# Attention times a gated FFN on one core: the place where softmax rows are divided by their sums, the engine that makes p's low part, and two narrow matmuls

## The chip, the cores and the metric

The kernel runs on one core of one Trainium2 chip. The metric is the device time of one launch in microseconds; the kernel before took 1223.08 us, the median of three runs (1222.31 to 1223.10). One more execution was taken with the hardware profiler. Engines are named as in the profile: PE is TensorE's matmul, PEld its weight load, DVE is VectorE, ACT is ScalarE, POOL is GpSimd, SP is SyncE, which here only issues transfers.

## The reference

x has 4 batches of 512 rows with 512 columns; there are 16 heads of 128 columns, and an FFN with 1408 inner columns whose weights are small integers (-1, 0, 1).

```python
xn = layernorm(x)                                  # no scale, no shift
q, k, v = (xn @ W + b for each of 16 heads)
scores = q @ k.T / sqrt(128), causal mask
attn = softmax(scores)                             # rows sum to 1
z = attn @ v
s = sum over heads of z @ W_O + b_O
g = silu(down(silu(xn @ gate * gate_s) * (xn @ up * up_s)) * down_s)
out = x + s * g
```

## The kernel before

Nearly every matrix is held as a high and a low part in a rounded 32-bit format (`Split`), and a product of two such matrices is three matmuls: high by low, high by high and low by high (`mm3`, lines 91 to 93). The high part is a cast, mostly on ACT, and the low part is the difference between the source and the high part, mostly on DVE; the low parts of the attention weights are made on POOL (`split_w`, line 135).

First the 512 rows of batch 0 are normalised and transposed. The later batches go the same way inside the first heads (`ln_stats`, `ln_normalize`, `ln_transpose`, `ln_low`).

Then the loop `heads` runs over 64 pairs of head and batch, n = 0 to 63: groups of two heads outermost (8 groups), the 4 batches next, the two heads of the group innermost (i = 0 and 1). The order of instructions is written out by hand. In one iteration TensorE does, in this order: the scores of this head (`softmax`, three packs of row tiles: the fourth, the third, the second with the first), two fillers (`fill`: for i = 0 the value projections psv of this batch and group, for i = 1 the output products pso of the previous one), the projections psq and psk for the next head, the value product of the previous head (`attend`, lines 376 to 393), and the other two fillers. So the probabilities of a head are used one iteration after they are made.

Between the scores and the value product, p goes this way. DVE masks, scales and takes the row maximum (L298); ACT exponentiates and sums the row (L312); DVE takes the reciprocal of the sum (L315) and POOL multiplies the row by it (L316). The row tiles are kept packed without the masked upper triangle: 10 tiles of 128x128. p has to be transposed: DVE transposes 32x32 blocks (L330, `turn_p`), one store writes them to device memory ("turn", L335) and four loads bring them back in the transposed order ("ptr", L341), all issued by SP. In the next iteration `split_p` makes the high part on ACT (L357) and the low part on DVE (L358), in two halves of 128x640 each. In the first heads (n < 4) and in the last iteration `split_p` stands right behind `softmax`, in the others behind the first fillers and the turn. For the very last head, TensorE transposes p instead (`transpose_p`, L370 and L372), as no iteration is left to hide the way through memory.

The value product has, for each of the four key tiles j, the rows from tile j on: widths 512, 384, 256 and 128. Each of the three parts (high by high, low by high, high by low) takes the four tiles, in the order 0, 3, 1, 2, into one PSUM tile z: 12 matmuls. ACT then adds the bias and rounds (L391, high part of z) and DVE makes the low part (L392).

The weights of the next group arrive through a pool of four raw buffers (`rawp`), by loads that ACT issues (L130), and are split when due (`split_pending`); q's and k's weights are split in the iterations n = 6, 14, ... (and 7, 15, ...). From group 1 on an output product adds to what is already in memory: ACT issues the load of it (L401), DVE adds (L413), SP issues the store (L414). ACT also issues loads of the FFN weights that are only examined (`load_look`, `look`).

PSUM has a ring of 3 buffers for scores and transposes (`ps_st`) and one of 5 for everything else (`ps_mm`): psq, psk, psv, pso, z, and half of the transposes of LN. A head takes seven buffers of the second ring.

After the last head come its value product, the four last output products, and the FFN: its weights are loaded by transfers that POOL issues (L651), gate and up products and then the down product for each batch.

Of the kernel before, what the change touches and what calls it, by code (L numbers as in the profile page):

```python
# [18 lines left out]
P = 128  # L19
HG = 2  # L20
# [22 lines left out]
def kernel(  # L43
# [21 lines left out]
    nc = tc.nc  # L65
    B, S, D = x.shape
# [29 lines left out]
    with ExitStack() as at:  # L96
# [111 lines left out]
        def ln_normalize(b, t):  # L208
            xt = x_in.pop((b, t))
            mv, sd = ln_of.pop((b, t))  # L210
            rstd = small.tile([P, 1], F32, name="rstd")
            nc.vector.reciprocal(rstd, sd)
            xn = lnp.tile([P, D], F32, name="xn")
            nc.vector.tensor_scalar(xn, xt, mv[:, 0:1], rstd, ALU.subtract, ALU.mult)
            xn_of[b, t] = xn

        def ln_transpose(b, t):
            xn = xn_of.pop((b, t))
# [53 lines left out]
        def softmax(qT, kT):  # L272
            p = pp.tile([P, NS * P], F32, name="p", tag="p")
            of = [p[:, row[t] : row[t] + (t + 1) * P] for t in range(NT)]
            nmax = {}
            for pack in PACK:
                sc = ps_st.tile([P, S], F32, name="sc", tag="st")
                at_ = 0
                where = {}
                for t in pack:  # L280
                    n = (t + 1) * P
                    where[t] = sc[:, at_ : at_ + n]
                    if t > 0:
                        mm3(where[t], qT[:, ts(t, P)], kT[:, :n], True, True)
                    at_ += n
                if 0 in pack:

                    two = sc[:, at_ - P : at_ + P]
                    nc.tensor.matmul(two, qT.hi[:, :P], kT.both[:, :, :P], start=True, stop=False)
                    nc.tensor.matmul(where[0], qT.lo[:, :P], kT.hi[:, :P], start=False, stop=True)  # L290
                for t in pack:
                    n = (t + 1) * P
                    add = mask[:, S - n :]
                    if t == 0:
                        add = small.tile([P, P], F32, name="add", bufs=1)
                        nc.vector.tensor_tensor(add, two[:, P:], mask[:, S - P :], ALU.add)
                    nmax[t] = small.tile([P, 1], F32, name="nmax", bufs=8)
                    nc.vector.tensor_tensor_reduce(  # L298
                        out=of[t],
                        in0=where[t],  # L300
                        in1=add,
                        scale=-SCALE,
                        scalar=BIG,
                        op0=ALU.add,
                        op1=ALU.min,
                        accum_out=nmax[t],
                    )
            for pack in PACK:
                for t in pack:
                    tot = small.tile([P, 1], F32, name="tot", bufs=8)  # L310
                    rtot = small.tile([P, 1], F32, name="rtot", bufs=8)
                    nc.scalar.activation(  # L312
                        of[t], of[t], AF.Exp, bias=nmax[t], scale=-1.0, accum_out=tot
                    )
                    nc.vector.reciprocal(rtot, tot)  # L315
                    nc.gpsimd.tensor_scalar(of[t], of[t], rtot, 1.0, ALU.mult, ALU.mult)  # L316
            return of

        def turn_p(of):

# [22 lines left out]
                )  # L343
            return raw

        def split_p(raw):
            pt = weight(pp, [P, NS, P], "pt", "pt")
            half = NQ // 2
            for k in range(0, NQ, half):
                src = raw[:, k : k + half].rearrange("p b (s i) -> p b s i", i=Q)  # L350

                def dst(part):
                    return part[:, :, k * Q : (k + half) * Q].rearrange(
                        "p s (b i) -> p b s i", i=Q
                    )

                nc.scalar.copy(dst(pt.hi), src)  # L357
                nc.vector.tensor_tensor(dst(pt.lo), src, dst(pt.hi32), ALU.subtract)  # L358
            return pt

        def transpose_p(of):

            pt = weight(pp, [P, NS, P], "pt", "pt")
# [12 lines left out]
        def attend(h, pt, vs):  # L376
            z = ps_mm.tile([P, NT, P], F32, name="z", tag="mm")


            todo = []  # L380
            for part, other in (("hi", "hi"), ("lo", "hi"), ("hi", "lo")):
                for j in (0, NT - 1, 1, 2):
                    v = getattr(vs[j], part)[:, ts(h % HG, E)]
                    p_ = getattr(pt, other)[:, slot[j] : slot[j] + NT - j, :]
                    todo.append((z[:, j:, :], v, p_))
            for k, (o, v, p_) in enumerate(todo):
                nc.tensor.matmul(o, v, p_, start=k == 0, stop=k == len(todo) - 1)  # L387
            zT = weight(zp, [P, NT, P], f"z{h}", "z")

            bias = bv_sb[:, h : h + 1]  # L390
            nc.scalar.activation(zT.hi, z, AF.Identity, bias=bias)  # L391
# [69 lines left out]
        with tc.manual_schedule():  # L461
# [56 lines left out]
            zs = {}  # L518
            inexact, before, raw = None, None, None

            def attend_last(before, pt):
                g, b, i = before
                zs.setdefault((g, b), []).append(attend(g * HG + i, pt, v_of[g, b]))

            for n, (g, b, i) in enumerate(heads):
                h = g * HG + i
# [22 lines left out]
                of = softmax(qT, kT)  # L549
                if n > 1 and early:  # L550
                    pt = split_p(raw)
                look()
# [1 line left out]
                fill(range(0, half))  # L554
                if nxt is not None:
                    raw_next = turn_p(of)
                if not early:
                    pt = split_p(raw)
                split_pending(n)
# [36 lines left out]
                    *_, kT = project(nxt[1], nh, wk[nh], bk_sb, "k")  # L596
                    raw = raw_next
                if before is not None:
                    attend_last(before, pt)
# [17 lines left out]
                before = g, b, i  # L617
# [6 lines left out]
            zs[last].append(attend(H - 1, pt, v_of[last]))  # L624
            for t in range(NT):
                project_out(*last, t, zs[last])

# [176 lines left out]
```

## Time and profile before

| what | value |
| --- | --- |
| median of three runs | 1223.08 us |
| the profiled execution | 1222.41 us |
| its span, from the first to the last instruction | 1220.6 us |
| scaling of p on POOL (L316) | 256 instructions, 598 ns mean |
| reciprocals on DVE (L315) | 256 instructions, 162 ns mean |
| low part of p on DVE (L358) | 126 instructions, 1099 ns mean |
| high part of p on ACT (L357) | 126 instructions, 724 ns mean |
| transposes of p on DVE (L330) | 378 instructions, 361 ns mean |
| packets below 512 bytes | 13232 of 117912 |
| mean transfer rate | 177 GB/s |

The span is the part of the execution between the first and the last instruction that the profile shows, and some 1.8 us lie around it. Busy time is the sum over an engine's instructions; matmuls overlap one another, so what a matmul costs is the distance between two starts and not its duration. A line of the timeline gives the start, the duration, the engine, the source line, the operation, what it writes and reads, and, in square brackets, the idle time of the engine just before it and what ended that.

### The profile page before, as it was taken

What the parts mean: (1) busy time and instruction counts of PE and PEld (TensorE: products, weight loads), DVE (VectorE), ACT (ScalarE), POOL (GpSimd) and SP (SyncE); (2) the same over time, 40 slices, a digit from 0 to 9 for tenths busy, and PEclk for the clock granted to TensorE, in tenths of its full rate; (3) what the DMA queues carried; (4) which work ended last, traced back from release to release, by engine and by line L of the source; (5) the groups of instructions that cost most, each with busy time, mean ns of one, the idle gap of its engine ahead of it and who ended that gap; (6) DMA issues with size and microseconds to landing.
All of it is one profiled execution on the core that took longest, in us unless ns stands there. A gap on an engine that the chain in (4) does not pass through costs nothing.

```text
span 1220.6 us, 18887 instructions
## 1 busy us (share of the span) xinstructions
PE 1206.5 (99%) x6514; PEld 1052.7 (86%) x6514; DVE 827.1 (68%) x2044; ACT 525.3 (43%) x1169; POOL 301.7 (25%) x433
## 2 busy tenths in 40 slices
PE   8999999999999999999999999999999999999997
PEld 8888888888888888888888888888888888888886
DVE  6897777777777777777877676767677533434343
ACT  5654444444445445444544454445444342323231
POOL 4212321232123213321412141214121341212010
PEclk9999999999999999999999999999999999999999
DMA  4454456656665667566655565555544893627241
GB/s 161 138 175 147 145 165 206 206 179 190 190 207 174 203 198 218 181 208 192 211 182 173 178 189 175 177 185 173 173 156 156 272 317 93 207 87 213 80 147 38
DMA packets 117912, 215.55 MB, mean 177 GB/s; under 512 B 13232, under 2 KB 45744, under 8 KB 117808
## 3 DMA queue, kind: packets, MB, share of 16 engines
q1 hardware_dynamic: 74016, 134.51, 34.4%
q10 hardware_dynamic: 29376, 53.26, 14.2%
q0 software_dynamic: 14416, 26.48, 7.9%
q8 instruction: 53, 0.87, 0.3%
q14 instruction: 51, 0.42, 0.1%
HBM read 135.17 MB, written 79.04 MB: 175 GB/s over the span
## 4 chain that ended last, share of the span: by engine, by line
PE 95%; DVE 3%; ACT 1%; DMA 0%; issue 0%; SPq 0%; DVEq 0%; ACTq 0%
PE z L387 10%; PE pd L667 7%; PE pg L667 7%; PE pu L667 7%; PE pso L91 5%; PE psv L91 5%; PE pso L92 5%; PE pso L93 5%; PE psv L93 5%; PE psv L92 5%; PE psq L91 5%; PE psq L92 5%; PE psq L93 5%; PE psk L91 5%; PE psk L92 5%; PE psk L93 5%
## 5 line engine op out<-in xcount | busy, mean ns | idle before, releaser
L316 POOL TENSOR_SCALAR p<-p,rtot 128x512 f32<-128x512 f32 (+3 forms) x256 | 148.2, 598 | 675.1 <-DVE rtot L315 675.1
L312 ACT ACTIVATE p<-p,nmax 128x512 f32<-128x512 f32 (+3 forms) x256 | 140.9, 552 | 147.3 <-DVE nmax L298 147.3
L358 DVE TENSOR_TENSOR ptl<-ptr,pth 128x640 fp32r<-128x640 f32 x126 | 133.7, 1099 | 1.4 <-ACT pth L357 1.4
L330 DVE STREAM_TRANSPOSE sq<-p 128x256 f32<-128x256 f32 x378 | 113.3, 361 | 0.0
L298 DVE CUSTOM_DVE_ANT_0 p<-sc,mask 128x512 f32<-128x512 f32 (+2 forms) x192 | 96.5, 552 | 0.3 <-PE sc L93 0.3
L252 ACT ACTIVATE k<-psk,consts 128x512 fp32r<-128x512 f32 (+1 forms) x65 | 44.2, 681 | 108.7 <-PE psk L93 108.6
L252 ACT ACTIVATE q<-psq,consts 128x512 fp32r<-128x512 f32 (+1 forms) x65 | 44.3, 682 | 97.2 <-PE psq L93 72.6
L357 ACT CAST pth<-ptr 128x640 fp32r<-128x640 f32 x126 | 84.9, 724 | 0.1
L413 DVE TENSOR_TENSOR a<-pso,a 128x512 f32<-128x512 f32 x108 | 72.1, 686 | 17.7 <-PE pso L93 16.4
L255 DVE SCALAR_TENSOR_TENSOR k<-psk,consts,k 128x512 fp32r<-128x512 f32 (+1 forms) x65 | 48.0, 739 | 52.8 <-ACT k L252 52.7
L693 DVE SCALAR_TENSOR_TENSOR hd<-pu,consts,sg 128x512 f32<-128x512 f32 x44 | 33.0, 751 | 66.8 <-PE pu L667 62.2
L315 DVE RECIPROCAL rtot<-tot 128x1 f32<-128x1 f32 x256 | 41.6, 162 | 42.7 <-ACT p L312 36.3
L91 PE MATMUL sc<-k,q 128*128 128x512 f32 (+2 forms) x192 | 65.7, 342 | 1.7 <-DVE xl L225 1.7
L93 PE MATMUL sc<-k,q 128*128 128x512 f32 (+2 forms) x192 | 64.7, 337 | 0.0
L92 PE MATMUL sc<-k,q 128*128 128x512 f32 (+2 forms) x192 | 64.7, 337 | 0.0
L255 DVE SCALAR_TENSOR_TENSOR q<-psq,consts,q 128x512 fp32r<-128x512 f32 (+1 forms) x65 | 47.6, 732 | 7.6 <-ACT q L252 7.6
L312 ACT ACTIVATION_READ_ACCUMULATOR p<-p,nmax 128x1 f32 x256 | 47.8, 187 | 0.0
L91 PEld LDWEIGHTS sc<-k,q 128*128 128x128 f32 x192 | 36.2, 188 | 7.9 <-DVE xl L225 3.5
L723 ACT ACTIVATE o<-o 128x512 f32<-128x512 f32 (+1 forms) x17 | 10.3, 607 | 68.8 <-DVE o L722 68.8
L92 PEld LDWEIGHTS sc<-k,q 128*128 128x128 f32 x192 | 36.2, 189 | 3.6
L93 PEld LDWEIGHTS sc<-k,q 128*128 128x128 f32 x192 | 36.1, 188 | 2.6
L691 ACT ACTIVATE sg<-pg,consts 128x512 f32<-128x512 f32 x44 | 30.3, 688 | 17.0 <-PE pg L667 17.0
(734 smaller groups left out, 3811.6 us busy)
## 6 DMA issues: line engine op xcount, KB each, us to landing
turn<-sq SPq DMA_DIRECT2D x63, 640.0 KB, 3.8
ptr<-turn SPq DMA_DIRECT2D x252, 160.0 KB, 3.4
acc<-a SPq DMA_DIRECT2D x124, 256.0 KB, 3.7
a<-acc ACTq DMA_DIRECT2D x108, 256.0 KB, 2.8
xt<-in_x SPq DMA_DIRECT2D x16, 256.0 KB, 4.1
wor<-in_w_o ACTq DMA_DIRECT2D x16, 256.0 KB, 4.5
fa<-acc SPq DMA_DIRECT2D x16, 256.0 KB, 5.9
fx<-in_x SPq DMA_DIRECT2D x16, 256.0 KB, 6.9
```

Of the source, the lines that this page charges most:

```text
L91: nc.tensor.matmul(ps, a.hi, b.lo, start=first, stop=False)
L92: nc.tensor.matmul(ps, a.hi, b.hi, start=False, stop=False)
L93: nc.tensor.matmul(ps, a.lo, b.hi, start=False, stop=last)
L252: nc.scalar.activation(q.hi[:, at_], ps[:, at_], AF.Identity, bias=bias[:, h : h + 1])
L255: nc.vector.scalar_tensor_tensor(q.lo[:, at_], ps[:, at_], bias[:, h : h + 1], q.hi32[:, at_], ALU.add, ALU.subtract,)
L298: nc.vector.tensor_tensor_reduce(out=of[t], in0=where[t], in1=add, scale=-SCALE, scalar=BIG, op0=ALU.add, op1=ALU.min, accum_out=nmax[t],)
L312: nc.scalar.activation(of[t], of[t], AF.Exp, bias=nmax[t], scale=-1.0, accum_out=tot)
L316: nc.gpsimd.tensor_scalar(of[t], of[t], rtot, 1.0, ALU.mult, ALU.mult)
L330: nc.vector.transpose(dst.rearrange("p a s i -> p s a i"), src.rearrange("p (s a i) -> p s a i", s=n, i=Q),)
L358: nc.vector.tensor_tensor(dst(pt.lo), src, dst(pt.hi32), ALU.subtract)
L387: nc.tensor.matmul(o, v, p_, start=k == 0, stop=k == len(todo) - 1)
L667: nc.tensor.matmul(ps, l, r, start=first and k == 0, stop=last and k == len(pairs) - 1)
```

## The change

Four things change.

p is no longer divided by its row sums. The four sums of a head are collected in one tile `tot`, one reciprocal is taken of all four, and the result is stored to a small memory tile in the order of the rows and loaded back as a row of 512 values that is repeated on all 128 partitions (`load_rtot`). The value product, whose columns are the query rows, is multiplied by it (`zn`), before bias and rounding.

p's low part is made on POOL instead of DVE. The high and low part now lie side by side in one tile (`p_split`).

The last key tile's matmuls leave the PSUM tile z. v's high part by both parts of p is one matmul of 256 columns, and v's low part by p's high part one of 128, into a tile z2 of its own; ACT copies z2 to the SBUF and DVE adds its two halves and then z. The other nine matmuls go in the order of the tiles.

The normalised rows of LN are written over x's tile instead of into one of their own.

```diff
-            xn = lnp.tile([P, D], F32, name="xn")
-            nc.vector.tensor_scalar(xn, xt, mv[:, 0:1], rstd, ALU.subtract, ALU.mult)
-            xn_of[b, t] = xn
+            nc.vector.tensor_scalar(xt, xt, mv[:, 0:1], rstd, ALU.subtract, ALU.mult)
+            xn_of[b, t] = xt
...
+            tot = small.tile([P, NT], F32, name="tot", bufs=2)
             for pack in PACK:
                 for t in pack:
-                    tot = small.tile([P, 1], F32, name="tot", bufs=8)
-                    rtot = small.tile([P, 1], F32, name="rtot", bufs=8)
                     nc.scalar.activation(
-                        of[t], of[t], AF.Exp, bias=nmax[t], scale=-1.0, accum_out=tot
+                        of[t], of[t], AF.Exp, bias=nmax[t], scale=-1.0,
+                        accum_out=tot[:, t : t + 1],
                     )
-                    nc.vector.reciprocal(rtot, tot)
-                    nc.gpsimd.tensor_scalar(of[t], of[t], rtot, 1.0, ALU.mult, ALU.mult)
-            return of
+            rtot = small.tile([P, NT], F32, name="rtot", bufs=2)
+            nc.vector.reciprocal(rtot, tot)
+            by_tile = dram.tile([NT, P], F32, name="rtot_d", tag="rtot_d", bufs=2)
+            nc.sync.dma_start(out=by_tile.rearrange("t p -> p t"), in_=rtot)
+            return of, by_tile
+
+        def load_rtot(by_tile):
+
+            r = small.tile([P, NT, P], F32, name="rb", bufs=2)
+            row_ = by_tile.rearrange("t p -> (t p)").rearrange("(o n) -> o n", o=1)
+            nc.sync.dma_start(
+                out=r.rearrange("p t q -> p (t q)"), in_=row_.broadcast_to([P, NT * P])
+            )
+            return r
...
+        def p_split():
+            both = pp.tile([P, 2, NS, P], F32R, name="pt", tag="pt")
+            pt = Split(both[:, 0], both[:, 1])
+            pt.both = both
+            return pt
...
                 nc.scalar.copy(dst(pt.hi), src)
-                nc.vector.tensor_tensor(dst(pt.lo), src, dst(pt.hi32), ALU.subtract)
+                nc.gpsimd.tensor_tensor(dst(pt.lo), src, dst(pt.hi32), ALU.subtract)
...
-        def attend(h, pt, vs):
+        def attend(h, pt, vs, rb):
             z = ps_mm.tile([P, NT, P], F32, name="z", tag="mm")
+            z2 = ps_mm.tile([P, 2, P], F32, name="z2", tag="mm")
+            last = NT - 1
+            e = ts(h % HG, E)
...
             for part, other in (("hi", "hi"), ("lo", "hi"), ("hi", "lo")):
-                for j in (0, NT - 1, 1, 2):
-                    v = getattr(vs[j], part)[:, ts(h % HG, E)]
+                for j in range(last):
+                    v = getattr(vs[j], part)[:, e]
...
+            s_ = slot[last]
+            nc.tensor.matmul(z2, vs[last].hi[:, e], pt.both[:, :, s_, :], start=True, stop=False)
+            nc.tensor.matmul(z2[:, 0], vs[last].lo[:, e], pt.hi[:, s_, :], start=False, stop=True)
+            zn = zp.tile([P, NT, P], F32, name="zn", bufs=1)
+            rest = small.tile([P, 2, P], F32, name="rest", bufs=1)
+            nc.scalar.copy(rest, z2)
+            nc.vector.tensor_tensor(rest[:, 0], rest[:, 0], rest[:, 1], ALU.add)
+            nc.vector.tensor_tensor(zn[:, last], z[:, last], rest[:, 0], ALU.add)
+            nc.vector.tensor_tensor(zn[:, :last], z[:, :last], rb[:, :last], ALU.mult)
+            nc.vector.tensor_tensor(zn[:, last], zn[:, last], rb[:, last], ALU.mult)
             zT = weight(zp, [P, NT, P], f"z{h}", "z")
...
-            nc.scalar.activation(zT.hi, z, AF.Identity, bias=bias)
-            nc.vector.scalar_tensor_tensor(zT.lo, z, bias, zT.hi32, ALU.add, ALU.subtract)
+            nc.scalar.activation(zT.hi, zn, AF.Identity, bias=bias)
+            nc.vector.scalar_tensor_tensor(zT.lo, zn, bias, zT.hi32, ALU.add, ALU.subtract)
...
                 if nxt is not None:
                     raw_next = turn_p(of)
+                rb_next = load_rtot(sums)
                 if not early:
                     pt = split_p(raw)
```

The sums' store is issued by SP behind the exponentials and ahead of the turn store of the same head; the repeated load behind the four ptr loads.

More of the change, by code (lines that the diff above doesn't have):

```diff
@@ L344, in turn_p @@
             return raw
+        def p_split():
[3 more added lines that the diff above has]
+            return pt
         def split_p(raw):
-            pt = weight(pp, [P, NS, P], "pt", "pt")
+            pt = p_split()
             half = NQ // 2
@@ L357, in split_p @@
                 nc.scalar.copy(dst(pt.hi), src)
[L358 removed]
+                nc.gpsimd.tensor_tensor(dst(pt.lo), src, dst(pt.hi32), ALU.subtract)
             return pt
         def transpose_p(of):
[L363 removed]
+            pt = p_split()
             pairs = [(j, t) for j in range(NT) for t in range(j, NT)]
@@ L519, with attend_last @@
             inexact, before, raw = None, None, None
-            def attend_last(before, pt):
+            def attend_last(before, pt, rb):
                 g, b, i = before
-                zs.setdefault((g, b), []).append(attend(g * HG + i, pt, v_of[g, b]))
+                zs.setdefault((g, b), []).append(attend(g * HG + i, pt, v_of[g, b], rb))
             for n, (g, b, i) in enumerate(heads):
@@ L548 @@
                     pt = split_p(raw)
-                of = softmax(qT, kT)
+                of, sums = softmax(qT, kT)
                 if n > 1 and early:
@@ L598 @@
                 if before is not None:
-                    attend_last(before, pt)
+                    attend_last(before, pt, rb)
                 if n == 1:
@@ L616 @@
                     fill(range(half, NT))
-                before = g, b, i
+                before, rb = (g, b, i), rb_next
                 if n == len(heads) - 4:
@@ L623 @@
             last = (NG - 1, B - 1)
-            zs[last].append(attend(H - 1, pt, v_of[last]))
+            zs[last].append(attend(H - 1, pt, v_of[last], rb))
             for t in range(NT):
```

## The prediction

> **What bounds the kernel now.** First the page's busy shares, then the chain of waits by engine:
>
> ```profile
> PE 1206.5 (99%) x6514; PEld 1052.7 (86%) x6514; DVE 827.1 (68%) x2044; ACT 525.3 (43%) x1169; POOL 301.7 (25%) x433
> ...
> PE 95%; DVE 3%; ACT 1%; DMA 0%; issue 0%; SPq 0%; DVEq 0%; ACTq 0%
> ```
>
> then the stage windows; this row covers some 16 of the 64 heads (n = 0 to 63; value products start 14.8 us apart); after the window stand its length and PE's busy time:
>
> ```profile
> 400.00:640.00 240.00, 240.00 (x1346) 212.17 (x1346) 183.66 (x468) 109.40 (x258) 64.72 (x80) 1.00 0.64 199
> ```
>
> TensorE is busy 240 of 240 us at full granted clock. So only two things count: TensorE work added or removed, and new TensorE stalls. DVE, ACT and POOL have room on average; I ask where a result of theirs now comes later than TensorE has work to bridge.
>
> **TensorE work.** One value product in the timeline (start, duration):
>
> ```profile
> 505.45 0.39 PE L387 MATMUL z<-pth,v_0h 128*128 128x512 f32 x1
> 505.68 0.22 PE L387 MATMUL z<-pth,v_3h 128*128 128x128 f32 x1
> 505.73 0.39 PE L387 MATMUL z<-pth,v_1h 128*128 128x384 f32 x1
> ...
> 507.36 0.28 PE L91 MATMUL psv<-wv4l,xh 128*128 128x256 f32 x1
> ```
>
> Durations overlap; the price is the pitch from start to start. The block takes 507.36 − 505.45 = 1.91. Pitches: 512 wide 0.23, 384 0.17, 256 0.12. A 128-wide matmul gives 0.055 here and makes the next one 0.055–0.06 later (its weight load isn't covered), together 0.115. The change turns three 128-wide ones into one 256-wide and one 128-wide: 3 × 0.115 − 0.118 − 0.115 = 0.11 a head. Four of 64 lie inside the stalls below: 60 × 0.112 = **−6.7 us**.
>
> **Other engines, per head.** POOL loses four scalings of p (598 ns mean, 2.1–2.5 us together) and gets two low parts of 128x640. The trace has no such POOL op; the nearest row is its 128x512 subtraction (second line: beside a DVE subtraction):
>
> ```profile
> 472.81 1.29 POOL L135 TENSOR_TENSOR wq8l<-wqr,wq8h 128x512 fp32r<-128x512 f32 x1 [1.49 <-ACT wq8h L134]
> 474.06 1.88 POOL L135 TENSOR_TENSOR wk8l<-wkr,wk8h 128x512 fp32r<-128x512 f32 x1
> ```
>
> By elements, 640/512 × 1.25 (pitch) = 1.57, the pair 3.15. Lower end: 2 × 1.25 = 2.5, if the instruction counts more than its elements; upper end: 640/512 × 1.88 = 2.35, the pair 4.7, if something beside it stretches it as the second line was. DVE loses 1.52 (the subtraction) and three of four reciprocals (3 × 0.16), and gets four operations after z: by its 128x128 add (0.29) and 128x384 and 512 rows (0.55, 0.69), 1.4. ACT gets one 128x256 copy (0.37). The copy, the four operations and their handovers put z's high part 2.4 us after the last matmul instead of 0.7, its low part 3.1 instead of 1.5, and each engine works in order: casts of v and additions of the output queued behind z come up to 1.7 later. The prediction rests on POOL's price, and here a rule speaks against the change. The Trainium skill, "GPSIMD Engine Reference", § 3.1 Elementwise, puts a two-input operation at about 2.6 cycles an element on GpSimd against one on DVE, and keeps elementwise work on DVE. By the row, 1.29 against DVE's 0.69 for 512, POOL takes 3.15; by the rule's 2.6 × 1.52, 4.0, an estimate. With 4.0 every stall below that waits for POOL grows by 0.85: 9 × 0.85 = 7.6 us more, an end of about 1234. I take the row.
>
> In most heads I expect no wait from either: in head 16 POOL's pair starts when ACT's first cast of p ends, 501.2, and ends at 504.4, and the z matmul that reads it, the seventh, comes at 506.6; z is read by the output product a head later; z's own PSUM buffer, the first of them to be used again, is due some 6 us on. Without that cover each us late is one us a head. Three places differ.
>
> **1. Heads 6, 14, ... 54 (seven).** Here POOL also makes wq's and wk's low parts (the two lines above), and ACT's queue holds loads that wait for their raw buffers:
>
> ```profile
> 471.49 0.73 ACT L357 CAST pth<-ptr 128x640 fp32r<-128x640 f32 x1
> ...
> 474.14 0.34 ACTq L130 DMA_DIRECT2D wqr<-in_w_q  x1
> 475.97 0.34 ACTq L130 DMA_DIRECT2D wkr<-in_w_k  x1
> 476.35 0.44 ACTq L438 DMA_DIRECT2D look<-in_up_w  x1
> 476.85 0.69 ACT L252 ACTIVATE q<-psq,consts 128x512 fp32r<-128x512 f32 x1 [3.59 <-PE psk L93]
> ```
>
> The load of wkr goes at 475.97, when POOL ends wk's low part (475.94); the cast of q stands behind it, so the releaser named, psk, is not what ended the wait. Now POOL does p's pair first: 471.73 to 474.87, then wq 1.25 to 476.12, wk 1.25 to 477.37 (nothing on DVE is beside it any more); q's high part 478.28, its low part until about 479.74. Before, that was hidden: no buffer was due. Now z2 takes an eighth PSUM buffer per head from a ring of five, so the second matmul group after z (due at 479.24) gets psq's buffer, released by q's low part: stall about 0.5. 7 × 0.5 = **+3.4 us**. With POOL's lower end nothing; with its upper end 0.5 + 1.55 = 2.05 a head.
>
> **2. The early heads (n = 1 to 3).** DVE runs from z0 without a gap into the next LN statistics and softmax:
>
> ```profile
> 46.32 0.69 DVE L187 BATCH_NORM_STATS2 st<-xt 128x6 f32<-128x512 f32 x1
> ...
> 49.52 0.66 DVE L298 CUSTOM_DVE_ANT_0 p<-sc,mask 128x512 f32<-128x512 f32 x1
> ```
>
> z0's longer chain moves all by 1.5. The exponentials and the cast of p follow, so z1 starts 1.5 later; POOL's pair then ends at 58.9, and the seventh matmul waits 1.3 more. q, LN, k, z1 and xl on DVE follow, and the third score product, which waits for xl already,
>
> ```profile
> 65.36 0.39 PE L91 MATMUL sc<-k,q 128*128 128x256 f32 x1 [0.41 <-DVE xl L225]
> ```
>
> comes at 68.15: **+2.8 us**; head 3 on has room.
>
> **3. The tail.** POOL's last pair ends at 962.3, where the seventh matmul was due at 961.66 (the new, shorter block wants it at 961.42); the casts for the last head's transposed p stand behind z14's longer chain on ACT, and the last value product ends at 968.45 instead of 966.70. Then nothing but one z14 group is left to cover z15's chain:
>
> ```profile
> 966.89 0.69 ACT L391 ACTIVATE z15h<-z,consts 128x512 fp32r<-128x512 f32 x1 [2.48 <-PE z L387]
> ```
>
> The first product with z15 went at 967.64, 0.94 after the block; now 2.45 after it: 970.9, **+3.25 us**.
>
> **Hidden.** The sums' 512-element store and 256 KB broadcast load go on SP: the store ahead of the turn store, the load behind the four ptr loads. Turn and ptr:
>
> ```profile
> turn<-sq SPq DMA_DIRECT2D x63, 640.0 KB, 3.8
> ptr<-turn SPq DMA_DIRECT2D x252, 160.0 KB, 3.4
> ```
>
> In head 16 ptr is issued until 508.36, lands about 511.8, and is needed at 514.17: 2.4 us of slack cover a delay. No row shows a store of single 4-byte elements; nearest by its kind is the 256 KB acc store, 3.7 to landing. The Trainium skill, "DMA: Bandwidth & Descriptors", § Rules for kernel authors, speaks against it: a last dimension that isn't contiguous goes as one descriptor an element, 512 here, and should be rearranged. By the row it lands 3.7 after its issue, which stands some 3 us ahead of the turn store, and turn loses under 1 us; by the rule it is dearer, without a price. Between nothing and 5 us I take the row: hidden. Beyond the slack every head pays (rival D). LN in place makes the next x load wait for the transposes instead of the normalising, far ahead of its use. The first FFN weight loads, behind POOL's last p work at 961.20, move past z15's chain too; the first lands some 2.6 us before its use: 0, at worst 1.
>
> **Sum.** −6.7 + 2.8 + 3.4 + 3.25 = +2.75 us on the profiled 1222.41: 1225.2; on the median of the three runs, 0.7 above that execution, 1225.8; I say **1226**. No change is within 0.2%, 2.45 us.
>
> **Rivals.**
> A, as summed, with its own range 1222 to 1231: 0.50.
> B, the other side: the stalls are covered. POOL's pair takes 2.6 or less, so that psq's buffer is free in time, and the early DVE queue catches up. Left are −6.7 + 2.5 of tail: 1219. It decides when POOL's chain in head 14 is 0.5 us shorter. For it: averages with much room. Against: POOL's row, and nothing shorter on it. 0.27.
> C, POOL's 32-element runs cost more than its contiguous row, 1.5 × 1.57 (the upper end): 7 × 2.05 + 4.35 + 4.8 − 6.7 = +16.8, 1240. DVE's pair shows no such penalty (0.76 each against 0.69 for 512). 0.13.
> D, the small store delays turn by over 2.4 us beyond its slack: each us is 60 us, 1280. 0.06.
> E, the joined matmul saves nothing, because its weight load stays exposed: +9.5, 1233. The 256-wide pitch 0.12 beside a 384 one speaks against. 0.04.
>
> The range 1220 to 1235 leaves out C, D and the lower part of B. Faster by over 0.2% (below 1220.6): 0.17 of B. Slower (above 1225.5): C, D, E and 0.32 of A, 0.55 in all. The rest, 0.18 of A and 0.10 of B, is 0.28.
>
> **What would show it.** Right: a z block of 1.80; waits of psv for q's low part in heads 6, 14, ...; a wait on POOL in the z block near 57 and 961; the third score product at 68. Wrong: POOL's op far from 1.57; a wait of pth for ptr; no stall in head 14.

## The result and the profile after

The changed kernel takes 1510.61 us (median of six runs, 1499.24 to 1521.22), the kernel before 1222.97 beside it: ratio 1.2355, 95% interval 1.2288 to 1.2422. The profiled execution has a span of 1518.1 us. The page of the changed kernel, busy shares, packets and the chain of waits by engine:

```profile
PE 1308.4 (86%) x6450; PEld 1103.4 (73%) x6450; DVE 746.8 (49%) x1982; ACT 541.5 (36%) x1233; POOL 330.0 (22%) x303
...
DMA packets 160921, 232.47 MB, mean 153 GB/s; under 512 B 48048, under 2 KB 80560, under 8 KB 160816
...
DMA 45%; PE 28%; DVE 11%; ACT 6%; SPq 3%; POOL 3%; issue 2%; ACTq 1%; DVEq 0%; POOLq 0%
```

TensorE, 95% of the chain before, is 28% of it now; transfers are 45%. The stage windows show TensorE idle for 54 of 300 us in the middle heads, at a granted clock of 0.91:

```profile
500.00:800.00 300.00, 246.15 (x1224) 207.64 (x1223) 148.87 (x422) 106.48 (x256) 65.15 (x46) 0.91 0.82 156
```

The transfers by kind (count, KB each, median us to landing) say which:

```profile
turn<-sq SPq DMA_DIRECT2D x63, 640.0 KB, 13.0
ptr<-turn SPq DMA_DIRECT2D x252, 160.0 KB, 3.4
acc<-a SPq DMA_DIRECT2D x124, 256.0 KB, 10.9
a<-acc ACTq DMA_DIRECT2D x108, 256.0 KB, 12.4
rb<-rtot_d SPq DMA_DIRECT2D x64, 256.0 KB, 4.6
...
rtot_d<-rtot SPq DMA_DIRECT2D x64, 2.0 KB, 12.7
```

The smallest store of the program, 2 KB, takes 12.7 us, and what starts beside it is late as well: turn lands in 13.0 us instead of 3.8, the loads of the output sums, which ACT issues, in 12.4. ptr and rb are issued when it is over, and ptr lands as before. The loads of the output sums in the kernel before:

```profile
a<-acc ACTq DMA_DIRECT2D x108, 256.0 KB, 2.8
```

One head in SP's timeline of the changed kernel:

```profile
587.50 0.38 SPq L318 DMA_DIRECT2D rtot_d<-rtot  x1
587.93 0.98 SPq L444 DMA_DIRECT2D acc<-a  x2
589.01 0.44 SPq L346 DMA_DIRECT2D turn<-sq  x1
603.29 1.91 SPq L352 DMA_DIRECT2D ptr<-turn  x4
```

turn goes out 1.5 us behind the store and ptr 14.3 us behind turn, because it reads what turn wrote. From there two ways lead to TensorE. The waits of the engines (total in us, times, longest):

```profile
ACT pt L374 <- DMA ptr<-turn: 189.4, 47, 11.8
...
ACT q L251 <- DMA rtot_d<-rtot: 105.2, 11, 10.4
...
PE z L407 <- ACT pt L374: 65.9, 34, 7.2
PE pso L91 <- DVE q L254: 62.5, 12, 6.4
...
PE z L407 <- POOL pt L375: 41.5, 43, 1.3
```

The first way is the long one, by turn and ptr: the casts of p wait for ptr, and the value product z waits for p's two parts. The second goes through ACT's own order. In the head shown ACT has cast p by 591.58 and issued four loads by 592.85, and then it stands until a load of FFN weights goes out at 601.21; q's cast comes behind that load:

```profile
601.64 0.69 ACT L251 ACTIVATE q<-psq,consts 128x512 fp32r<-128x512 f32 x1 [10.06 <-DMA rtot_d<-rtot]
```

The trace puts this wait down to the 2 KB store itself, which lands at 601.19. The load doesn't touch what the store writes; in the trace both report their landing on one semaphore (the counter that tells that a transfer is done), and the load's issue waits for it. TensorE waits for q's low part, and after the wait goes on slowly:

```profile
596.64 0.39 PE L93 MATMUL pso<-wo3h,z7l 128*128 128x512 f32 x1
603.17 0.80 PE L91 MATMUL pso<-wo3l,z6h 128*128 128x512 f32 x1 [6.14 <-DVE q L254]
603.76 0.63 PE L92 MATMUL pso<-wo3h,z6h 128*128 128x512 f32 x1
604.19 0.63 PE L93 MATMUL pso<-wo3h,z6l 128*128 128x512 f32 x1
```

Matmuls of 512 columns are 0.43 us apart there instead of 0.23, and TensorE stays slow for some 6 us: from 603.10 to 609.10 its granted clock is 0.52.

### The profile page after: what moved, and what is told of

It reads as the page before. It is cut to its first block, busy times and chain, and to the rows that moved or that the text cites. A ratio compares the mean times of both kernels' runs of the same rounds, so it can differ in the third digit from the quotient of the medians.

```text
span 1518.1 us, 18901 instructions
## 1 busy us (share of the span) xinstructions
PE 1308.4 (86%) x6450; PEld 1103.4 (73%) x6450; DVE 746.8 (49%) x1982; ACT 541.5 (36%) x1233; POOL 330.0 (22%) x303
## 4 chain that ended last, share of the span: by engine, by line
DMA 45%; PE 28%; DVE 11%; ACT 6%; SPq 3%; POOL 3%; issue 2%; ACTq 1%; DVEq 0%; POOLq 0%
DMA turn<-sq 23%; DMA rtot_d<-rtot 10%; PE pd L698 5%; PE pg L698 5%; PE pu L698 5%; DMA ptr<-turn 5%; DMA a<-acc 5%; DVE sq L341 3%; ACT p L311 3%; SPq L352 3%; POOL pt L375 2%; DMA acc<-a 1%; DVE a L443 1%; PE pso L91 1%; PE psv L91 1%
## 5 line engine op out<-in xcount | busy, mean ns | idle before, releaser
L375 POOL TENSOR_TENSOR pt<-ptr,pt 128x640 fp32r<-128x640 f32 x126 | 193.6, 1558 | 959.9 <-ACT pt L374 932.3
L407 PE MATMUL z<-pt,v_0h 128*128 128x512 f32 x128 | 66.6, 520 | 115.3 <-ACT pt L374 65.9
L374 ACT CAST pt<-ptr 128x640 fp32r<-128x640 f32 x126 | 85.3, 725 | 189.9 <-DMA ptr<-turn 189.4
L407 PEld LDWEIGHTS z<-pt,v_0h 128*128 128x128 f32 x128 | 26.3, 205 | 145.5 <-ACT pt L374 82.0
L251 ACT ACTIVATE q<-psq,consts 128x512 fp32r<-128x512 f32 (+1 forms) x65 | 44.1, 678 | 188.2 <-DMA rtot_d<-rtot 105.2
L91 PE MATMUL sc<-k,q 128*128 128x512 f32 (+2 forms) x192 | 72.2, 376 | 6.7 <-DVE xl L224 4.5
L92 PE MATMUL sc<-k,q 128*128 128x512 f32 (+2 forms) x192 | 70.2, 365 | 0.0
L93 PE MATMUL sc<-k,q 128*128 128x512 f32 (+2 forms) x192 | 69.3, 361 | 0.0
L91 PEld LDWEIGHTS sc<-k,q 128*128 128x128 f32 x192 | 41.0, 214 | 14.6 <-DVE xl L224 6.3
L407 PE MATMUL z<-pt,v_1h 128*128 128x384 f32 x128 | 48.9, 382 | 0.0
L413 ACT COPY rest<-z 128x256 f32<-128x256 f32 x64 | 23.9, 373 | 68.2 <-PE z L410 57.3
L316 DVE RECIPROCAL rtot<-tot 128x4 f32<-128x4 f32 x64 | 11.4, 178 | 73.3 <-ACT p L311 73.3
L414 DVE TENSOR_TENSOR rest<-rest 128x128 f32<-128x128 f32 x64 | 22.7, 355 | 48.6 <-ACT rest L413 48.6
## 6 DMA issues: line engine op xcount, KB each, us to landing
a<-acc ACTq DMA_DIRECT2D x108, 256.0 KB, 12.4
```

The source lines that it names most:

```text
L91: nc.tensor.matmul(ps, a.hi, b.lo, start=first, stop=False)
L92: nc.tensor.matmul(ps, a.hi, b.hi, start=False, stop=False)
L251: nc.scalar.activation(q.hi[:, at_], ps[:, at_], AF.Identity, bias=bias[:, h : h + 1])
L375: nc.gpsimd.tensor_tensor(dst(pt.lo), src, dst(pt.hi32), ALU.subtract)
```

## Experiments

The theory behind the first four, S: the 512-piece store delays the transfers. Rivals: P, p's low part on GpSimd and the longer chain of z; L, the repeated load of 256 KB.

### The trip of the sums taken away, and made cheaper

The changed kernel without the store and without the load, so that the division is left out (e1_no_trip):

```diff
-            nc.sync.dma_start(out=by_tile.rearrange("t p -> p t"), in_=rtot)
-            return of, by_tile
+            return of, None
...
-            r = small.tile([P, NT, P], F32, name="rb", bufs=2)
...
-            return r
+            return ones_rb
```

> The changed kernel without the sums' store and without the load that repeats them: the value product is multiplied by a constant tile of ones, so the division by the row sums is left out, and everything else of the change stays. Theory S (the 512 pieces of 4 bytes hold the transfer engines, and turn, ptr and the loads of the output sums come late): the time falls to what the prediction summed for the rest, 1226 us (1222 to 1231), turn lands in about 4 us again. Rival P (p's low part on GpSimd and the longer way from z to its high part are what stalls TensorE): it stays above 1400 us. Rival L (the 256 KB repeated load is to blame): 1226 us too, which the next runs tell apart.

Measured: 1239.53 us, ratio 1.0147 (1.0130 to 1.0164). Of the 287.6 us the trip is 271; rival P falls for these. But 17 us are left where 3 were expected, which the later runs follow.

The same store in 128 pieces of 16 bytes, in an order in which the columns get the sums of other rows (e2_pieces128):

```diff
-            by_tile = dram.tile([NT, P], F32, name="rtot_d", tag="rtot_d", bufs=2)
-            nc.sync.dma_start(out=by_tile.rearrange("t p -> p t"), in_=rtot)
+            by_tile = dram.tile([P, NT], F32, name="rtot_d", tag="rtot_d", bufs=2)
+            nc.sync.dma_start(out=by_tile, in_=rtot)
```

> The changed kernel with the same 2 KB stored in the order they lie in, 128 pieces of 16 bytes instead of 512 of 4; the load is unchanged, so the columns are divided by the sums of other rows. Theory S, if the price goes by pieces: a quarter of some 9 to 10 us, the store lands in about 4 us, turn loses 2.3 us at most, which its slack of 2.4 covers: 1226 to 1245 us. If the price goes by bytes or by the transfer as a whole, nothing changes: about 1500. Rival L: about 1500. Rival P: above 1400.

Measured: 1238.33 us, ratio 1.0129 (1.0112 to 1.0146), no more than without any trip; the store lands in 3.5 us, turn in 3.7. The load of 256 KB costs nothing that shows: rival L falls.

```profile
turn<-sq SPq DMA_DIRECT2D x63, 640.0 KB, 3.7
...
rtot_d<-rtot SPq DMA_DIRECT2D x64, 2.0 KB, 3.5
```

With the reciprocals turned in 32x32 blocks first (e3_pieces16), the division is whole again and the store has 16 pieces, in four transfers:

```diff
-            nc.vector.reciprocal(rtot, tot)
-            nc.sync.dma_start(out=by_tile.rearrange("t p -> p t"), in_=rtot)
+            nc.vector.reciprocal(rtot[:, :NT], tot)
+            turned = small.tile([P, Q], F32, name="rturn", bufs=2)
+            nc.vector.transpose(turned, rtot)
+            for a in range(NQ):
+                nc.sync.dma_start(out=by_tile[:, ts(a, Q)], in_=turned[a * Q : a * Q + NT, :])
```

> The changed kernel with the sums' reciprocals turned in 32x32 blocks on VectorE first, so that the store is 16 pieces of 128 bytes, issued as four transfers. Theory S by pieces: the store lands in 2 to 3 us, the time is that of the run without the trip or 1 to 3 us above it, 1224 to 1232. Rival L: about 1500, as the repeated load is still there. Rival P: above 1400.

Measured: 1239.75 us, ratio 1.0146 (1.0128 to 1.0163): the trip is free, the rest stays 8 us above the range.

### The store alone, in the kernel before

e4_store_alone adds only the store, e13_store256 half of it, e14_store_spread all of it with its pieces apart:

```diff
+            by_tile = dram.tile([NT, P], F32, name="rtot_d", tag="rtot_d", bufs=2)       # e4
+            nc.sync.dma_start(out=by_tile.rearrange("t p -> p t"), in_=rtots)
...
+            by_tile = dram.tile([2, P], F32, name="rtot_d", tag="rtot_d", bufs=2)        # e13
+            nc.sync.dma_start(out=by_tile.rearrange("t p -> p t"), in_=rtots[:, :2])
...
+            by_tile = dram.tile([P, NT, P], F32, name="rtot_d", tag="rtot_d", bufs=2)    # e14
+            nc.sync.dma_start(out=by_tile[:, :, 0], in_=rtots)
```

> The kernel before with nothing but the 512-piece store of the reciprocals added (nobody reads what it stores). Theory S: 64 heads of about 4.5 us more, 1450 to 1550 us, turn's landing from 3.8 to about 13 us. Rivals P and L: 1223 to 1230 us.

Measured: 1438.55 us, ratio 1.1702 (1.1627 to 1.1778). A store that nobody reads costs 216 us. Most of TensorE's waits come by turn and ptr (ACT's casts of p wait 272.1 us for ptr, and the value products 120.6 for the casts); 21.1 us of ACT's waits, six in all, are put down to the store itself.

> The kernel before with a store of the reciprocals of two of the four tiles a head, 256 pieces of 4 bytes, read by nobody. Price by pieces (512 take about 10 us, 128 take 3.5): it lands in 5 to 6 us and turn in some 5 to 7; with 2.4 us of slack in the middle heads 1223 to 1290 us. If the time of the store does not go by its pieces: about 1438 us as with 512.

Measured: 1444.91 us, ratio 1.1841 (1.1812 to 1.1869). Half the pieces, the same price: a price by pieces falls.

> The kernel before with the store of all four reciprocals, 512 pieces of 4 bytes, but each to a place of its own 512 bytes from the next, instead of side by side. Price by pieces, wherever they go: it lands in about 10 us, 1420 to 1470 us. Rival N (the price comes from many small writes into the same 512 bytes of memory): it lands in 3 to 4 us, 1223 to 1240 us.

Measured: 1228.94 us, ratio 1.0057 (1.0040 to 1.0074). The transfers by kind of the run with 512 pieces side by side (e4), of that with 256 side by side (e13) and of that with 512 spread (e14), each turn and then the store:

```profile
turn<-sq SPq DMA_DIRECT2D x63, 640.0 KB, 11.1
...
rtot_d<-rtot SPq DMA_DIRECT2D x64, 2.0 KB, 10.4
```

```profile
turn<-sq SPq DMA_DIRECT2D x63, 640.0 KB, 11.3
...
rtot_d<-rtot SPq DMA_DIRECT2D x64, 1.0 KB, 10.1
```

```profile
turn<-sq SPq DMA_DIRECT2D x63, 640.0 KB, 4.1
...
rtot_d<-rtot SPq DMA_DIRECT2D x64, 2.0 KB, 2.9
```

As many pieces as small as before land in 2.9 us once each has 512 bytes to itself: what counts is what lies beside a piece and not how many there are, as rival N has it. In e4 and e13 each row of 512 bytes takes 128 single writes, whether there are four rows or two, and both take 10 us, which is 80 ns a write if the rows go side by side and the writes of a row one after another (a reading; the distance was 4 or 512 bytes and nothing between, so the size of the stretch that is shared isn't known, nor whether it counts that e14's pieces lie spread over 256 KB in all). In e2 a row takes 32 writes.

### What is left: the parts one by one

The 17 us of the kernel with the cheap store. The low part of p back on VectorE (e5_low_on_vector), and the kernel before with one part of the change each: the join (e6_join_alone), GpSimd (e7_gpsimd_alone), the division (e8_division_alone).

```diff
-                nc.gpsimd.tensor_tensor(dst(pt.lo), src, dst(pt.hi32), ALU.subtract)         # e5
+                nc.vector.tensor_tensor(dst(pt.lo), src, dst(pt.hi32), ALU.subtract)
...
-                nc.vector.tensor_tensor(dst(pt.lo), src, dst(pt.hi32), ALU.subtract)         # e7
+                nc.gpsimd.tensor_tensor(dst(pt.lo), src, dst(pt.hi32), ALU.subtract)
...
+            nc.scalar.copy(rest, z2)                    # e6: nine matmuls into z, two into z2
+            nc.vector.tensor_tensor(rest[:, 0], rest[:, 0], rest[:, 1], ALU.add)
+            nc.vector.tensor_tensor(zn, z[:, last], rest[:, 0], ALU.add)
...
+            nc.vector.tensor_tensor(zn, z, rb, ALU.mult)                                     # e8: 12 matmuls
```

> The run with the 16-piece store (1239.75 us), but p's low part is made on VectorE again; the division behind the value product and the joined matmuls stay. In that run the value product takes 1.77 us instead of 1.91, but psq and psk matmuls, 512 wide, come 0.2333 us apart instead of 0.2270, which gives 24 x 0.0063 = 0.15 us a head back. Theory G (GpSimd's 3.1 us a head on p cause the waits for q's low part, 7.1 us, the waits of the value product near 57 and 972, 2.4 us, and also the wider pitch, 9.6 us): 1220 us and a pitch of 0.227. Rival H (the wider pitch comes from the joined matmuls or from where the tiles lie now, not from GpSimd): 1230 us, and the pitch stays at 0.233. Rival Z (the longer way from z to its high part makes the waits): 1238 us or more.

Measured: 1244.29 us, ratio 1.0180 (1.0163 to 1.0197): 4.5 us more than with GpSimd. Theory G falls: the time isn't shorter, and the pitch stays at 0.233. TensorE's waits in this run (total, times, longest) have a new first line:

```profile
PE z L411 <- DVE pt L379: 4.8, 7, 1.3
```

VectorE, with the new operations of z and p's low part besides, is late for the value product seven times. With GpSimd (e3) TensorE waits for p's low part twice, 2.2 us in all.

> The kernel before with nothing but the joined matmuls: a tile z2, p's two parts side by side, the last 128 columns of z added on VectorE; the division and the low part of p stay as they were. Theory G: the value product takes 1.77 us, all else keeps its pitch: 60 x 0.14 = 8.4 us less, 1 to 2 us more at the beginning and at the end: 1214 to 1217 us. Rival H, if joined matmuls or side-by-side parts are its cause: psq and psk at 0.233, and 1222 to 1226 us.

Measured: 1222.46 us, ratio 1.0003 (0.9994 to 1.0011), though value products now start 14.67 and 14.69 us apart in the middle heads (before: 14.78 and 14.81), 0.11 less, with psq and psk still at 0.227. The gain is given back: 3.3 us are lost by the third value product (77.51 us, before 74.22), 0.2 to 0.6 in each of five middle heads, and z15's chain makes TensorE wait 1.1 at the end.

> The kernel before with nothing but p's low part on GpSimd. Theory G: no eighth buffer, so q's low part may be late unseen, but the early heads wait 1.3 us and the end 1 us, and psq and psk go to 0.233: 60 x 0.15 = 9 us; 1232 to 1236 us. Rival H: the pitch stays at 0.227, 1223 to 1226 us.

Measured: 1223.78 us, ratio 1.0013 (1.0006 to 1.0019). The middle heads are as before (1.91, 14.78, 14.81), the pitch is 0.227, and the only waits for GpSimd are the two foreseen ones, 2.1 us. Its two operations take 3.1 us a head, and that is hidden.

> The kernel before with nothing but the division moved behind the value product, by the 16-piece store and the repeated load (and LN in place, for room): 12 matmuls as before, p's low part on VectorE, nothing on GpSimd but weights. Theory G: the chain behind z grows by 0.7 to 0.8 us, 1 us at the beginning and 1 us at the end: 1223 to 1225 us, pitch 0.227. Rival H by the place of the tiles: pitch 0.233 and 1232 to 1235 us.

Measured: 1234.43 us, ratio 1.0097 (1.0081 to 1.0114), twelve us for a part that adds no TensorE work; some six of them are lost evenly, head by head, in the middle. TensorE's timeline of the kernel before and of this run, inside one psk:

```profile
532.55 0.39 PE L92 MATMUL psk<-xh,wk9h 128*128 128x512 f32 x1
532.78 0.39 PE L93 MATMUL psk<-xh,wk9l 128*128 128x512 f32 x1
533.00 0.39 PE L91 MATMUL psk<-xl,wk9h 128*128 128x512 f32 x1
533.23 0.39 PE L92 MATMUL psk<-xh,wk9h 128*128 128x512 f32 x1
```

```profile
539.58 0.39 PE L93 MATMUL psk<-xh,wk9l 128*128 128x512 f32 x1
539.81 0.40 PE L91 MATMUL psk<-xl,wk9h 128*128 128x512 f32 x1
540.05 0.39 PE L92 MATMUL psk<-xh,wk9h 128*128 128x512 f32 x1
540.28 0.40 PE L93 MATMUL psk<-xh,wk9l 128*128 128x512 f32 x1
```

Three pitches are 0.68 before and 0.70 here, with no wait in either. 24 such matmuls a head would make 0.15 us; the periods grow by 0.06 and 0.15 (14.87 and 14.93). TensorE is busy in both; a busy share doesn't show this, only the starts do.

### The place of the tiles

The edits change the size of the pools, so the weight tiles lie elsewhere in the SBUF. Padding puts them back: 4032 bytes a partition in e9 (the division alone) and 752 words, 3008 bytes, in e12 (the changed kernel with the 16-piece store). The 448 bytes of e15 leave them 3584 bytes off. In these three the small tiles that the turn of the reciprocals reads lie in the padded pool too. e10_ln_in_place moves them without touching a middle head.

```diff
+            pad = small.tile([P, 1008], F32, name="pad", bufs=1)     # e9; 112 in e15, 752 in e12
+            nc.gpsimd.memset(pad, 0.0)
...
-            xn = lnp.tile([P, D], F32, name="xn")                    # e10
-            nc.vector.tensor_scalar(xn, xt, mv[:, 0:1], rstd, ALU.subtract, ALU.mult)
+            nc.vector.tensor_scalar(xt, xt, mv[:, 0:1], rstd, ALU.subtract, ALU.mult)
```

> The division alone (1234.43 us; psq and psk 0.230 to 0.239 us apart in place of 0.227, and no wait in the middle heads) with 4032 bytes a partition put in, so that the weights, q, k, v and all tiles behind them lie where they lie in the kernel before. Theory W (the wider pitch comes from where the weight tiles lie against x's): the pitch is 0.227 again, the period of a head 14.80, and the time 1225 us (1223 to 1227). Rival E (it comes from what the other engines do beside it: the longer chain of z, the load of the repeated sums): pitch and time stay, 1233 to 1236 us.

Measured: 1230.80 us, ratio 1.0066 (1.0051 to 1.0081); pitch 0.227, periods 14.78 and 14.81 as before the change. Inside one psk, three pitches are 0.68 again:

```profile
536.70 0.39 PE L91 MATMUL psk<-xl,wk9h 128*128 128x512 f32 x1
...
537.38 0.39 PE L91 MATMUL psk<-xl,wk9h 128*128 128x512 f32 x1
```

The pitch is theory W's; the time is above its range, since the beginning (4.4 us by the third value product) and the end (3.3) cost more than I had put down. At both places a wait of TensorE (2.0 and 1.4 us) is followed by 3.4 us at half the clock (granted 0.50 from 67.4 and from 975.4), which the kernel before has at neither.

> The kernel before with nothing but LN written over x's tile, which moves the weights and all tiles behind them by 8192 bytes a partition. Theory W: the pitch of psq and psk can change though no instruction of the middle heads does; at 0.233 it would be 1232 us; if this distance happens to be as good as the old one, 1222 us. Rival E: 1222 to 1223 us and 0.227.

Measured: 1222.20 us, ratio 0.9999 (0.9991 to 1.0008), pitch 0.227: this move does no harm.

> The division alone once more (1234.43 us), now with 448 bytes a partition put in instead of 4032: the weights don't come back to their old places, but lie 3584 bytes, seven times 512, from them. So far the pitch of 0.227 was kept where they moved by 0, 1536 or 8192 bytes, and lost where they moved by 192, 3264, 3456, 4288 or 7552 against x's tiles. If a multiple of 512 is what counts: 0.227, a period of 14.80, and 1231 us as with the old places. If only the old places themselves or multiples of larger powers of two do: 0.230 or more, 14.90, and 1234 us.

Measured: 1230.27 us, ratio 1.0065 (1.0046 to 1.0085), pitch 0.227. Of all kernels here, those whose weight tiles lie a multiple of 512 bytes from where they were, against x's tiles, have 0.227 (0, 1536, -3584, -8192), and the others 0.233. These shifts are worked out from the sizes of the tiles in each edit. From 400 to 900 us, without the stretches at half clock, the average pitch is 0.2273 in all eight of the first kind, the kernel before among them; it is 0.2328 in the three whose shift leaves a rest of 128 bytes over a multiple of 512, and 0.2333 in the six with a rest of 320. What makes it so the runs don't show. One of the six is e14, with a shift of -192: its periods are 14.87 and 14.93 and its 6.8 us over the kernel before are mostly this, not its store.

> The changed kernel with the 16-piece store (1239.75 us), and with 3008 bytes a partition put in so that the weights and all behind them lie where they lie in the kernel before. Theory W: psq and psk 0.227 apart again, the period of a middle head 14.68 instead of 14.82, 58 x 0.15 = 8.7 us less: 1231 us (1229 to 1233), of which the rest over the kernel before, some 9 us, is the waits at the beginning, at the heads with wq and wk, and at the end, less the join's 6.4. If the place did not matter here: 1239 us.

Measured: 1232.64 us, ratio 1.0092 (1.0074 to 1.0110), pitch 0.227, periods 14.67 and 14.69. The place was worth 7.1 us of the 17.

### A version that keeps the gain

e11_join_middle has the join alone, only where there is room for its chain, with z2 in the ring of three and p's low part on GpSimd there:

```diff
+            if join:            # heads 3 to 61
+                z2 = ps_st.tile([P, 2, P], F32, name="z2", tag="st")
...
-                    pt = split_p(raw)
+                    pt = split_p(raw, nc.gpsimd)
...
-                    attend_last(before, pt)
+                    attend_last(before, pt, not early)
```

> The kernel before with the joined matmuls only where there is room: the heads from the fourth on but the last two, z2 in the ring of three buffers of the scores instead of the ring of five, p's low part of these heads on GpSimd; no division, no LN in place. The first heads and the end are as before. If the join is worth 0.11 us a head (its run alone had a period of 14.68) and the waits came from the eighth buffer and from the early and last heads: 58 x 0.11 = 6.4 us less, 1216 us (1215 to 1218). If z2 or the chain of z brings a new wait: 1220 or more.

Measured: 1216.48 us, ratio 0.9957 (0.9943 to 0.9971): 5.8 us less than before, the value product 1.76, the periods 14.67 and 14.69. The division stays where it was in the kernel before. TensorE is as full as before the change in the window:

```profile
400.00:640.00 240.00, 239.95 (x1338) 211.89 (x1337) 161.09 (x487) 117.50 (x293) 109.28 (x112) 1.00 0.62 196
```

## Where the prediction was right and where it failed

**The step that failed** is the one under "Hidden": "Between nothing and 5 us I take the row: hidden." The row, acc's store of 256 KB, was near in queue and issuer but not in what decides, the size and the neighbours of the single writes. The store takes 12.7 us instead of 3.7 and delays turn by 9.2, where "turn loses under 1 us" stood, against 2.4 of slack. The sign of being wrong that the prediction named, a wait of p's cast for ptr, came: 189.4 us. A second way it didn't ask about: the store also holds up what ACT issues, and with it q's cast, 105.2 us in 11 waits. Rival D named this case; its 0.06 was far too little, and the range left it out, though the one rule that the prediction weighed here spoke for it: without any row for single 4-byte writes, the upper end had no ground at 5 us. The rule of the Trainium skill, "DMA: Bandwidth & Descriptors", § Rules for kernel authors, gave the right warning; its ground, one descriptor an element, is not the whole price, as 512 elements that lie apart land in 2.9 us. The same page's Specifications say that transfers under 512 bytes go by read-modify-write; writes that queue for one such stretch would fit the runs, which show the price and not the mechanism.

The clock makes it dearer. TensorE's busy time is 1308.4 us for 6450 matmuls; without the trip (e1) it is

```profile
PE 1212.7 (98%) x6450; PEld 1049.8 (85%) x6450; DVE 742.4 (60%) x1982; ACT 541.3 (44%) x1233; POOL 332.9 (27%) x304
```

for as many, at a mean granted clock of 0.993 instead of 0.924. The two spans are 281 us apart (1518.1 and 1236.7): 96 of these are slower matmuls, the other 186 idle time. Rival D's 60 us for each us beyond the slack would give (9.2 − 2.4) × 60, some 400. Why the heads pay less than that the runs don't show.

**The other steps**, read from the changed kernel with cheap store and old places (e12):

- The join: 60 × 0.112 = 6.7 us predicted; the period falls by 0.11 in each middle head, 58 × 0.11 = 6.4. Right. Rival E, that the joined matmul saves nothing, is out.
- POOL's pair: 3.15 us predicted from the 128x512 row, 3.1 measured (1558 ns an operation on the page). Right, and rival C falls with it. The 4.0 set against it counted a cycle of GpSimd as long as one of VectorE: by the ratio of 1.96 that the Trainium skill, "GPSIMD Engine Reference", § 3.1 Elementwise, gives as measured for a two-input addition, it would be 1.96 × 1.52 = 2.98, an estimate near what came. The rule to keep such work on VectorE doesn't hold in this kernel, where VectorE has the new operations of z: the move to GpSimd saves 4.5 us (e3 against e5). In the kernel before it costs 1.5 (e7).
- Heads 6, 14, ... 54: the mechanism is right. Without the trip (e1), head 38, GpSimd's timeline, then ACT's and TensorE's:

```profile
599.16 3.10 POOL L368 TENSOR_TENSOR pt<-ptr,pt 128x640 fp32r<-128x640 f32 x2 [13.78 <-ACT pt L367]
...
603.49 1.28 POOL L135 TENSOR_TENSOR wk10l<-wkr,wk10h 128x512 fp32r<-128x512 f32 x1
```

```profile
604.80 0.34 ACTq L130 DMA_DIRECT2D wkr<-in_w_k  x1
...
605.67 0.69 ACT L251 ACTIVATE q<-psq,consts 128x512 fp32r<-128x512 f32 x1 [4.91 <-PE psv L93]
```

```profile
605.27 0.28 PE L93 MATMUL psv<-wv4h,xl 128*128 128x256 f32 x1
607.19 0.39 PE L91 MATMUL psv<-wv4l,xh 128*128 128x256 f32 x1 [1.64 <-DVE q L254]
```

  The second psv after z waits for psq's buffer, as foreseen. The size was off: these heads are 0.43 to 1.40 us longer than the others, 5.8 in all instead of 3.4 (7.1 in e1), because the pair starts 3.0 us ahead of z (599.16 against 602.15) where I had 4.1 (471.73 against 475.86): in e1 VectorE goes from z's longer chain without a gap into the softmax, whose exponentials stand ahead of the casts of p on ACT (read from the timelines, not tried alone).
- The early heads: 2.8 us predicted, 4.5 measured (third value product at 78.67 instead of 74.22). The two waits are the ones foreseen, 1.5 for p's cast and 1.2 for GpSimd. Not foreseen was what comes with them, a stretch of 6.9 us at half the clock, where the kernel before had 1.00:

```profile
57.05 0.50 PE L411 MATMUL z<-pt,v_0h 128*128 128x512 f32 x1 [1.55 <-ACT pt L378]
59.58 0.79 PE L411 MATMUL z<-pt,v_0h 128*128 128x512 f32 x1 [1.21 <-POOL pt L379]
```

```profile
58.90:65.80 6.90, 6.22 (x27) 6.12 (x28) 6.55 (x18) 1.27 (x4) 3.29 (x3) 0.51 0.51 167
```

  That is worth some 3 us, an estimate (half the stretch), and some waits of before fall away. The division alone (e9) and the join alone (e6) lose 4.4 and 3.3 there with nothing of p on GpSimd, by a wait of 2.0 for VectorE and 3.4 us at half the clock: z's longer chain is enough for the loss.
- The tail: 3.25 predicted, 4.0 measured: the FFN's first matmul comes 7.5 us later in the profile (981.47, before 974.00) and 3.5 of it are there at the last value product but two (953.18, before 949.68). The waits are the ones named: 1.0 for GpSimd, 0.6 for the cast of the last head's p, 1.9 for z15.
- The first FFN weights: their load moves behind z15's chain, and the wait before the first gate matmul stays 0.9 us. Right.
- Not in the sum: the place of the tiles, 7.1 us. No step asked what the new pool sizes do to a matmul that the change doesn't touch.

With the old places the terms make −6.4 + 5.8 + 4.5 + 4.0 = 7.9 us, and the profiled execution of e12 is 8.3 longer than that of the kernel before (spans 1228.9 and 1220.6). Its median is 10.5 us above the kernel before; the two us between stay open.

## What to carry to other kernels

A store's cost isn't in its bytes: before a small result goes through memory, count its separate writes and how many lie side by side, and where no row of the trace shows such a store, take no upper end for it. Turning it on the chip first, so that it leaves in a few long pieces, made the same trip free here. When no wait is new and the time has grown all the same, compare the pitch of matmuls that weren't touched: here pools of another size had moved the weights, and padding that set them a multiple of 512 bytes from their old places gave 7 us back. And a wait can cost more than itself: look at the granted clock behind it.

## What the runs showed of the hardware that was not expected

- 256 or 512 single writes of 4 bytes side by side take 10 us and hold up transfers of both issuing queues; 512 of them, each 512 bytes from the next, land in 2.9 us.
- A transfer can hold up the issue of one that has nothing to do with it, on another engine, where both report on one semaphore: ACT's load at 601.21 waits for SP's store, which lands at 601.19.
- The pitch of 512-column matmuls depends on where the weights lie against the moving data: 0.2273 us on average at multiples of 512 bytes from the old distance, 0.2328 or 0.2333 otherwise, at a granted clock of 1.00 in both.
- After some waits TensorE is granted half its clock (0.50 to 0.52) for 3.4 to 6.9 us, and 512-column matmuls are 0.43 us apart: after 6.1 us in the changed kernel (603.10 to 609.10), after a wait of 1.5 us and from within one of 1.2 in the early heads of e12 (58.9 to 65.8), after 1.9 us in the tail of e1 (983.5 to 986.9), after 1.4 us in that of e9 (975.4 to 978.8). After the 1.6 us of head 38 in e1 and the 1.9 us in the tail of e12 it isn't. What decides wasn't tried.
- VectorE's addition of two SBUF halves, 128x128, takes 0.28 us, and 0.67 while GpSimd works on weights (e1, at 607.71 and at 621.31).
